# Layer 1 of a two-layer graph attention kernel: when a half block's sums are scaled and transposed

## The chip, the core and the metric

The kernel runs on one core of one Trainium2 chip. The metric is device time in microseconds (us) of one execution; of several runs the median is taken. A core has five engines that run side by side and hand work on through semaphores: TensorE (PE: matrix products, and transposes done as products), VectorE (DVE: element-wise work and reductions), ScalarE (ACT: copies with a scale, and functions such as exp), GpSimd (POOL: here mainly the issue of gathers and scatters by index) and SyncE (SP: here the issue of plain transfers). Transfers run on 16 DMA engines.

## The reference

Two graph attention layers over N = 2708 nodes with 1024 features, one adjacency matrix `adj`, and after each layer a residual sum and a layer norm:

```python
def _L1_gnn_ref(input, adj, W, a1, a2):
    h = input @ W
    f1 = h @ a1
    f2 = h @ a2
    e = jax.nn.leaky_relu(f1 + f2.T, negative_slope=0.2)
    scores = jnp.where(adj > 0, e, neg)
    attention = jax.nn.softmax(scores, axis=1)
    h_prime = attention @ h
    return jax.nn.relu(h_prime)

x = _layernorm(x + _L0_gnn_ref(x, adj, Wf, bf, Wg, bg, W0, bW))
x = _layernorm(x + _L1_gnn_ref(x, adj, W1, a1, a2))
```

Layer 0 differs in its scores (a product of two projections). The change concerns layer 1 alone. A row of `adj` has few ones, so the kernel turns it into lists of neighbours first and from then on works on listed neighbours only.

## The kernel before

**Preparation and layer 0** (lines 106 to 1105). The kernel reads `adj`, makes for each node a list of its neighbours, sorts nodes by the length of the list, and runs layer 0. Layer 0 leaves in DRAM the rows that layer 1 reads: table `T1` (1028 numbers a row: the 1024 features of layer 0's output and its product with a2's vector in column 1024) and `X1S` (the same rows as residual). The weight of layer 1 stands in `M` in SBUF.

**Layer 1: blocks, parts and tiles.** Sorted nodes form 22 blocks: one of 32 rows (20 of them real) and 21 of 128. A block of 128 has four groups of 32 rows; a *part* is half of it, two groups (`ks` = (0,1) or (2,3)). The small block is one part. That gives 43 parts, 0 to 42 here, in the order of `parts` (line 1193): part 0 is the small block, parts 2j-1 and 2j are the halves of the j-th block after it. A *tile* is one neighbour slot of one group: 128 gathered rows of T1 (526 KB). A part has 3 to 14 tiles, the last fourteen parts ten each; 405 in all.

**Gathers.** POOL issues one gather for each tile, into one of 33 slots: 20 in `ring` and 13 in `more`. The gather of tile m + 33 may go once the sums have read tile m. `Layer.gathers` (line 669) is called after each part's sums and issues those whose slots are named free then, that of the tile read last ahead of the others.

**One part, step by step.** The names are those of the profile:

- `scores1(u, ks)` (line 1137), DVE: takes column 1024 of each tile (`scores<-ring`, `scores<-more`), adds the row's own term, leaky relu and mask; then `Halves.soft` (line 776): the maximum over a row's four partitions, the difference, exp on ACT (`scores<-scores`), two multiplies that spread the weights into the stationary operand (`st<-scores,stack`), the row sums and their reciprocals (`ri`).
- `lay.sums` (line 815), TensorE: the weighted sums of the gathered rows (`po<-ring,st`, `po<-more,st`), into one of two PSUM banks in turn (`banks[:, n % 2]`).
- `lay.out` (line 839), ACT: the sums times the reciprocals, from PSUM to SBUF (`y<-po,ri`). The buffer of `y` has two copies.
- `turn_half` and `lay.turn` (lines 1207, 844): four transposes of `y` on TensorE (`pt<-ident,y`), then copies into `yT` on ACT (`yT<-pt`).
- When both halves of a block are turned, two `piece`s (line 1201) follow: half of the block's product with `M` each, eight products of 128x512 (`pm<-M,yT`; the profile counts each as two records). One part's iteration does one piece.
- `close1` (line 1157), after the second piece: SP loads the residual (`rb`, `u1b` or `u2b<-X1S`), DVE adds it to relu of the product, makes mean and variance and a Newton step for the root, ACT scales (`rb<-rb,sh,rstd`), and POOL scatters the rows to the output (`out_dram<-rb,ids`), which is issued one iteration later, ahead of that iteration's gathers.

**Order.** Each engine takes its instructions in the order in which the program names them; the class `InOrder` (line 61) holds them to it. So the order of the lines in the loop at line 1215 is the order of the queues. In iteration n it is:

- TensorE: sums(n), a piece, the transposes of part n-1
- ACT: exp(n+1), y(n), the copies of part n-1's transposes, the scale of a closing block
- DVE: scores of part n+1, the closing block's sum and norm
- POOL: the scatter of the block closed in iteration n-1, then gathers

A block whose second part is n is turned wholly in iteration n+1, has its two pieces in n+2 and n+3, closes in n+3 (an odd number) and is scattered in n+4. After the loop stand what is left: the last piece of the block before the last, the transposes of the last part, the product of the last block (`two_products`, line 557, sixteen products) and its close.

Some memsets of a small table on POOL, a count on DVE and TensorE in part 24, and the load of a flag in part 40 stand in the same loop; they serve a check of the lists' lengths.

Of the kernel before, what the change touches and what calls it, by code (L numbers as in the profile page):

```python
# [8 lines left out]
F32 = mybir.dt.float32  # L9
# [97 lines left out]
def listed_path(ctx, tc, x, adj, Wf, bf, Wg, bg, W, bW, W1, a1, a2, out):  # L107

    nc = tc.nc
    P = 128  # L110
    N, D = x.shape
    KC = D // P
    H = D // 512
# [83 lines left out]
    with tc.tile_pool(name="pre", bufs=1) as pre:  # L197
# [54 lines left out]
        with tc.tile_pool(name="adjp", bufs=3) as adjp, tc.tile_pool(name="cands", bufs=2) as cands, \  # L252
# [184 lines left out]
            steps = weights()  # L437
# [82 lines left out]
    def turn(rows, n, dst, halves=False):  # L520


        pts = []
        for k0 in range(0, KC, 4):
            pt = ps_t.tile([P, 4, P], F32, name="pt")
            at = slice(64, 64 + n) if halves and k0 and n < P else slice(0, n)
            for k in range(4):
                pe.transpose(pt[:, k, :n], rows[at, (k0 + k) * P:(k0 + k + 1) * P], ident[at, at])
            pts.append(pt)
        yield  # L530
        for k0, pt in zip(range(0, KC, 4), pts):
            if halves and k0 and n == P:
                for a, b in ((0, 64), (64, 0)):
                    act.copy(dst[:, k0:k0 + 4, a:a + 64], pt[:, :, b:b + 64])
            else:
                act.copy(dst[:, k0:k0 + 4, :n], pt[:, :, :n])
# [14 lines left out]
    def half_product(pm, h, n, xT, w, row=None):  # L551
        c = slice(h * 512, (h + 1) * 512)
        for k in range(KC):
            pe.matmul(pm[:n, h, :], xT[:, k, :n], w[:, k, c],
                      start=(row is None and k == 0), stop=(k == KC - 1))
# [43 lines left out]
    def scatter(table, idx, src):  # L599
        pool.indirect_dma_start(  # L600
            out=table, out_offset=bass.IndirectOffsetOnAxis(ap=idx, axis=0), in_=src,
            in_offset=None, bounds_check=N - 1, oob_is_err=False)

    def norm(z, n, made=None):


        st = small.tile([P, H, 6], F32, name="bst")
        mv = small.tile([P, 2], F32, name="mv")
        for h in range(H):
            if made is not None:  # L610
                made(h)
            dve.bn_stats(st[:n, h, :], z[:n, h * 512:(h + 1) * 512])
        dve.bn_aggr(mv[:n], st[:n])
        var, r, t = (small.tile([P, 1], F32, name=s) for s in ("var", "rstd", "newton"))
        dve.tensor_scalar(var[:n], mv[:n, 1:2], EPS, None, op0=ALU.add)
        ri, ti = r.bitcast(I32), t.bitcast(I32)
        dve.tensor_scalar(ti[:n], var.bitcast(I32)[:n], 1, None, op0=ALU.logical_shift_right)
        dve.tensor_scalar(ri[:n], ti[:n], -1.0, float(0x5F3759DF), op0=ALU.mult, op1=ALU.add)
        for _ in range(3):
            dve.tensor_scalar(t[:n], var[:n], r[:n], r[:n], op0=ALU.mult, op1=ALU.mult)  # L620
            dve.tensor_scalar(t[:n], t[:n], -0.5, 1.5, op0=ALU.mult, op1=ALU.add)
            dve.tensor_scalar(r[:n], r[:n], t[:n], None, op0=ALU.mult)
        sh = small.tile([P, 1], F32, name="sh")
        dve.tensor_scalar(sh[:n], mv[:n, 0:1], r[:n], -1.0, op0=ALU.mult, op1=ALU.mult)
        yield
        act.activation(z[:n, :D], z[:n, :D], AF.Identity, bias=sh[:n], scale=r[:n])
# [242 lines left out]
    with ExitStack() as s0s:  # L869
# [3 lines left out]
        stp, xp, yp, jp = (new_pool(n, 1) for n in ("stp0", "xp", "yp", "jp0"))  # L873
# [3 lines left out]
        lay = Layer(units, [ring], D, x, stp)  # L877
        xb, q, qd, F, Fr, xTs, yTs, Wp, y, Z = ({} for _ in range(10))
# [53 lines left out]
        def close(b):  # L932

            n, m, z = nrows[b], valid[b], Z.pop(b)
            pm = Wp.pop(b)

            def add(h):
                c = slice(h * 512, (h + 1) * 512)
                dve.tensor_add(z[:n, c], pm[h][:n, h, :], z[:n, c])

            if b + 1 < NB:
                dve.tensor_add(z[:n, :D], flat(pm)[:n], z[:n, :D])
            steps = norm(z, n, None if b + 1 < NB else add)
            next(steps)
            yield
            for _ in steps:
                pass
            sp.dma_start(X1S[start[b]:start[b] + m, :], z[:m, :D])
            yield
            dot(z[:n, :D], u2b, n, z[:n, D:D + 1])  # L950
            dot(z[:n, :D], u1b, n, f1[:n, b:b + 1])
            yield
            if z is not zs:
                pool.memset(z[:, D + 1:], 0.0)
            scatter(T1[:, :], ids[:m, b:b + 1], z[:m])
# [43 lines left out]
        for ks in ((0, 1), (2, 3)):  # L999
            for h in range(H):  # L1000
                c = slice(h * 512, (h + 1) * 512)
# [22 lines left out]
        closing, loaded = iter(()), 3  # L1024
        for k, u in enumerate(units):
            nxt = units[k + 1] if k + 1 < len(units) else None
            b = u.b
# [4 lines left out]
            po = ps_s.tile([P, H, 512], F32, name="po")  # L1032
# [22 lines left out]
            closing = iter(())  # L1055
# [24 lines left out]
            steps = turn(y[b], nrows[b], yT, halves=True)  # L1080
# [13 lines left out]
            if back is not None:  # L1094
                closing = close(back)
                next(closing)
        b = NB - 1
# [10 lines left out]
    with ExitStack() as s1s:  # L1108
        new_pool = lambda name, bufs: s1s.enter_context(tc.tile_pool(name=name, bufs=bufs))
        tp, yp = (new_pool(n, 2) for n in ("tp1", "yp1"))  # L1110
# [10 lines left out]
        lay = Halves(units, [ring, more], TW, T1[:, :], stp)  # L1121
# [35 lines left out]
        def close1(b, pm):  # L1157
            m, z = valid[b], x1[done1[b] % 3]
            sp.dma_start(z[:m], X1S[start[b]:start[b] + m, :])
            last = b == order1[-1]  # L1160

            def add(h):
                c = slice(h * 512, (h + 1) * 512)
                dve.scalar_tensor_tensor(z[:m, c], pm[h][:m, h, :], 0.0, z[:m, c], op0=ALU.max, op1=ALU.add)

            if not last:
                dve.scalar_tensor_tensor(z[:m], flat(pm)[:m], 0.0, z[:m], op0=ALU.max, op1=ALU.add)
            for _ in norm(z, m, add if last else None):
                pass
            yield  # L1170
            scatter(out, ids[:m, b:b + 1], z[:m])
# [4 lines left out]
        def mark_over(b):  # L1176

            for g in groups[b]:
                if g == 0:
                    for q in range(Q):  # L1180
                        pool.memset(over[32 * q:32 * q + valid[0], 0, TILES[0]:], 1.0)
                elif TILES[g] < QT:
                    pool.memset(over[:, g, TILES[g]:], 1.0)
# [10 lines left out]
        lay.gathers()  # L1194
        pool.memset(over, 0.0)
        scores1(*parts[0])
        closing, pieces, turning = iter(()), [], None
        banks = ps_s.tile([P, H, 512], F32, name="po")
        yT = {}

        def piece(b, h, pm):
            if h == 0:
                pm.append(ps_m.tile([P, H, 512], F32, name="pm"))
            half_product(pm[0], h, nrows[b], yT[b], M)
            return (b, pm[0]) if h + 1 == H else None

        def turn_half(u, ks, y):
            b = u.b
            if ks[0] == 0:
                yT[b] = tp.tile([P, KC, P], F32, name="yT")  # L1210
            steps = lay.turn(y, ks, yT[b])
            next(steps)
            return steps

        for n, (u, ks) in enumerate(parts):
            b, po = u.b, banks[:, n % 2, :]
            latest = lay.sums(u, po, ks)
            for _ in closing:
                pass
            closing = iter(())  # L1220
            lay.gathers(latest)
            made = pieces.pop(0)() if pieces else None
            steps = iter(())
            if turning is not None:
                v, kv, _ = turning
                steps = turn_half(*turning)
                if kv[-1] + 1 == v.G:
                    pm = []
                    pieces += [lambda c=v.b, h=h, pm=pm: piece(c, h, pm) for h in range(H)]
            if n + 1 < len(parts):  # L1230
                scores1(*parts[n + 1])
            y = yp.tile([P, 512], F32, name="y1")
            lay.out(u, po, ks, y)
            for _ in steps:
                pass
            turning = u, ks, y
            if ks[-1] + 1 == u.G:
                k = done1[b]
                for i in (2 * k, 2 * k + 1):
                    if i < NB:  # L1240
                        mark_over(i)
                if k == NB // 2 + 1:
                    count_over()
                if k + 2 == NB:
                    unfit = nc.values_load(flag[0:1, 0:1])
            if made is not None:
                closing = close1(*made)
                next(closing)
        while pieces:
            made = pieces.pop(0)()  # L1250
        for _ in turn_half(*turning):
            pass
        for _ in closing:
            pass
        closing = close1(*made)
        next(closing)
        prod = two_products(P, yT[b], M)
        for _ in closing:
            pass
# [366 lines left out]
```

## Time and profile before

| | us |
|---|---|
| median of 3 runs | 1890.39 |
| lowest and highest run | 1887.95, 1898.44 |
| profiled execution | 1750.29 |
| its span, first to last instruction | 1748.6 |
| layer 1's first gather starts at | 1133.72 |
| layer 1's last gather starts at | 1686.89 |
| last part's sums start at | 1700.09 |
| last scatter starts at | 1740.15 |

Of the span, PE is busy 1563.6 us (89%), DVE 1297.5 (74%), POOL 1180.9 (68%) and ACT 643.5 (37%). By stretches of layer 1, with the busy time of each engine (x: instructions), the TensorE clock that was granted, the DMA engines' busy share and what they moved in GB/s:

```
1133.00:1249.00 116.00, 89.60 (x408) 32.25 (x408) 65.30 (x326) 15.19 (x35) 88.92 (x120) 0.88 0.97 366
1249.00:1465.00 216.00, 197.97 (x955) 84.67 (x956) 126.89 (x603) 32.25 (x72) 166.77 (x222) 0.98 1.00 384
1465.00:1650.00 185.00, 169.09 (x829) 69.78 (x828) 111.70 (x531) 27.23 (x63) 141.42 (x144) 0.96 1.01 389
1650.00:1700.00 50.00, 44.55 (x200) 18.85 (x198) 27.75 (x144) 7.35 (x16) 28.64 (x29) 0.97 0.81 309
1700.00:1748.60 48.60, 33.39 (x114) 14.08 (x112) 15.97 (x52) 6.23 (x10) 2.93 (x3) 0.88 0.09 34
```

The columns after the length are PE (products), PE's weight loads, DVE, ACT and POOL.

How to read a line of the timeline: start, duration, engine, source line (all of layer 1 goes through one helper, L71, so the names of the tiles tell the instructions apart), operation, what is written and read, its shape, how many were merged, and in brackets how long the engine stood idle before and what ended that. A line of the groups has the count, then the busy time and the mean in ns, then the idle time before it and what ended that. A wait for several semaphores is put down to the one that came last. A gather's time on POOL is its issue; the transfer lands later.

### The profile page before, as it was taken

To read this page: it belongs to the slowest core of one execution; us is meant where nothing else is said; L and a number is where in the kernel's file an instruction comes from. 1 tells how busy PE (TensorE), PEld (TensorE's weight loads), DVE (VectorE), ACT (ScalarE), POOL (GpSimd) and SP (SyncE) were. 2 spreads that over 40 slices of the span, in tenths; PEclk is the share of its full clock that TensorE was granted. 3 is DMA by queue.
4 is the path that set the end of the run, shared out by engine and by line. 5 is a ranking of instruction groups with operands and counts; after the bars stand their busy time and mean duration, and the time that the engine had idled before them with its cause. 6 is when DMAs were issued, how large, how long until landed. Compare 5 with 4: busy or idle time off the path is not lost. (4 is left out here: it accounts for less than half of the span.)

```text
span 1748.6 us, 23112 instructions
## 1 busy us (share of the span) xinstructions
PE 1563.6 (89%) x6969; PEld 675.5 (39%) x6969; DVE 1297.5 (74%) x4262; ACT 643.5 (37%) x902; POOL 1180.9 (68%) x1195
## 2 busy tenths in 40 slices
PE   4999578899999999999999999559899888999896
PEld 2444233344444444444444444213344333343332
DVE  5879846899999989998999977547465555665652
ACT  4555455444444554555554444101111111111111
POOL 7888476467667767776677743177777777777740
PEclk8999778999999999999999999879999999999998
DMA  7656168578877777888887876399999999999960
GB/s 287 228 185 236 38 232 309 199 252 292 302 277 283 269 253 276 294 293 284 303 299 285 291 267 249 121 394 357 367 374 392 391 397 375 384 392 390 396 253 38
DMA packets 149986, 502.80 MB, mean 288 GB/s; under 512 B 32340, under 2 KB 32372, under 8 KB 147144
## 3 DMA queue, kind: packets, MB, share of 16 engines
q0 software_dynamic: 132032, 428.29, 66.2%
q1 hardware_dynamic: 10202, 55.72, 8.4%
q10 hardware_dynamic: 7618, 17.23, 2.7%
q8 instruction: 57, 0.93, 0.2%
q14 instruction: 77, 0.63, 0.1%
HBM read 509.64 MB, written 33.75 MB: 311 GB/s over the span
## 5 line engine op out<-in xcount | busy, mean ns | idle before, releaser
L71 POOL DMA_INDIRECT ring<-in_x_dram,SL x405 | 429.9, 1062 | 164.0 <-issue 70.0
L71 DVE SCALAR_TENSOR_TENSOR j<-ring,Fr 128x1024 bf16<-128x1024 f32 x402 | 493.9, 1229 | 41.1 <-DMA ring<-in_x_dram,SL 13.9
L71 PE MATMUL po<-ring,st 128*32 128x512 f32 x2616 | 324.4, 616 | 56.9 <-ACT y L71 32.5
L71 ACT COPY Fr<-pm 32x1024 f32<-32x1024 f32 (+2 forms) x353 | 340.6, 965 | 18.8 <-PE pm L71 14.1
L71 PE MATMUL pm<-M,yT 128*128 128x512 f32 (+1 forms) x704 | 313.3, 598 | 0.5 <-ACT yT L71 0.5
L71 PE MATMUL pm<-Wt,xT 128*128 128x512 f32 (+1 forms) x704 | 300.5, 599 | 4.7 <-DMA Wt<-in_L_gnn_W_dram 4.7
L71 POOL DMA_INDIRECT ring<-T,SL x249 | 247.0, 992 | 80.5 <-issue 66.3
L71 PE MATMUL pm<-M,xT 128*128 128x512 f32 x672 | 297.5, 601 | 0.0
L71 ACT ACTIVATE scores<-scores 128x12 f32<-128x12 f32 (+9 forms) x65 | 14.0, 216 | 631.6 <-DVE scores L71 631.6
L71 PEld LDWEIGHTS pm<-M,yT 128*128 128x128 f32 (+1 forms) x704 | 127.8, 186 | 185.0 <-issue 183.8
L71 PEld LDWEIGHTS pm<-Wt,xT 128*128 128x128 f32 (+1 forms) x704 | 131.0, 189 | 163.4 <-issue 154.6
L71 PEld LDWEIGHTS pm<-M,xT 128*128 128x128 f32 x672 | 130.2, 194 | 158.0 <-issue 155.1
L71 POOL DMA_INDIRECT more<-T,SL x156 | 154.6, 991 | 48.5 <-issue 43.8
L71 PEld LDWEIGHTS po<-ring,st 128*32 128x32 f32 x2616 | 95.9, 113 | 229.8 <-issue 174.0
L412 POOL TENSOR_TENSOR adj<-adj,iota 128x2708 f32<-128x2708 f32 (+3 forms) x23 | 130.6, 5685 | 22.7 <-ACT adj L71 22.6
L415 DVE MAX8 cand<-adj 128x8 f32<-128x136 f32 (+2 forms) x440 | 97.2, 285 | 37.4 <-POOL adj L412 37.4
L71 PE MATMUL pm<-halfT,WfT 128*128 128x512 f32 x256 | 114.1, 601 | 1.1 <-ACT WfT L71 1.1
L71 POOL DMA_INDIRECT SL<-LD,idq x85 | 86.4, 1016 | 25.8 <-issue 24.0
L71 PE MATMUL po<-more,st 128*32 128x512 f32 x624 | 82.4, 625 | 14.3 <-ACT y L71 14.3
L71 DVE TENSOR_SCALAR scores<-ring,f1q 128x4 f32<-128x4 f32 (+6 forms) x69 | 16.5, 245 | 104.1 <-DMA ring<-T,SL 93.1
L71 POOL DMA_INDIRECT z<-in_x_dram,ids x21 | 24.0, 1142 | 87.1 <-DVE j L71 36.4
L71 PEld LDWEIGHTS pm<-halfT,WfT 128*128 128x128 f32 x256 | 48.2, 193 | 58.0 <-issue 55.2
(214 smaller groups left out, 1539.5 us busy)
## 6 DMA issues: line engine op xcount, KB each, us to landing
adj<-in_adj_dram SPq DMA_DIRECT2D x21, 1354.0 KB, 5.8
X1S<-z SPq DMA_DIRECT2D x19, 512.0 KB, 5.2
ring<-in_x_dram,SL POOLq DMA_INDIRECT x405, 6.5
rows<-in_L_gnn_Wg_dram ACTq DMA_DIRECT2D x8, 512.0 KB, 4.4
rows<-in_L_gnn_Wf_dram ACTq DMA_DIRECT2D x8, 512.0 KB, 3.5
rows<-in_L_gnn_W_dram ACTq DMA_DIRECT2D x8, 512.0 KB, 6.1
Wt<-in_L_gnn_W_dram ACTq DMA_DIRECT2D x1, 4096.0 KB
M<-in_L_gnn_W_dram SPq DMA_DIRECT2D x1, 4096.0 KB
```

The source lines that it names most:

```text
L71: made = self.tc.keep_in_program_order(op(*args, **kwargs))
L412: nc.gpsimd.tensor_tensor(k[:n, cut], k[:n, cut], iota[:n, cut], op=ALU.mult)
L415: nc.vector.max(cand[:n, s, :], k[:n, s * SEG:min((s + 1) * SEG, N)])
```

## The change

The call that copies a part's sums out of PSUM (`lay.out`) moves ahead of the next part's scores, and the part's own transposes are made in the same iteration, after the piece; the variable that held a part back for the next iteration (`turning`) goes, and so does what followed the loop for it.

```diff
-        closing, pieces, turning = iter(()), [], None
+        closing, pieces = iter(()), []
...
             lay.gathers(latest)
+            y = yp.tile([P, 512], F32, name="y1")
+            lay.out(u, po, ks, y)
             made = pieces.pop(0)() if pieces else None
-            steps = iter(())
-            if turning is not None:
-                v, kv, _ = turning
-                steps = turn_half(*turning)
-                if kv[-1] + 1 == v.G:
-                    pm = []
-                    pieces += [lambda c=v.b, h=h, pm=pm: piece(c, h, pm) for h in range(H)]
+            steps = turn_half(u, ks, y)
+            if ks[-1] + 1 == u.G:
+                pm = []
+                pieces += [lambda c=b, h=h, pm=pm: piece(c, h, pm) for h in range(H)]
             if n + 1 < len(parts):
                 scores1(*parts[n + 1])
-            y = yp.tile([P, 512], F32, name="y1")
-            lay.out(u, po, ks, y)
             for _ in steps:
                 pass
-            turning = u, ks, y
...
-        while pieces:
-            made = pieces.pop(0)()
-        for _ in turn_half(*turning):
-            pass
-        for _ in closing:
-            pass
-        closing = close1(*made)
-        next(closing)
         prod = two_products(P, yT[b], M)
```

The queues of iteration n afterwards:

- TensorE: sums(n), a piece, the transposes of part n
- ACT: y(n), exp(n+1), the copies of part n's transposes, the scale of a closing block
- DVE: scores of part n+1, the closing block's sum and norm
- POOL: the scatter of the block closed in iteration n-1, then gathers

A block whose second part is n has its pieces in n+1 and n+2, closes in n+2 (an even number) and is scattered in n+3. After the loop stand the product of the last block and its close.

## The prediction

> **What bounds the kernel now.** I read the page's slices first, then the groups of layer 1, then POOL's timeline from 1133 us to the end, then TensorE's and ACT's timelines beside it. The change touches layer 1 alone, which starts with the first `ring<-T,SL` gather at 1133.72. A "part" is half a block of rows; layer 1 has 43 of them, 0 to 42.
>
> ```profile
> PE   4999578899999999999999999559899888999896
> POOL 7888476467667767776677743177777777777740
> DMA  7656168578877777888887876399999999999960
> ```
>
> From slice 27 on POOL stands at an even 7, the DMA engines at 9, TensorE between 8 and 9. An even 7 on POOL is not slack:
>
> ```profile
> L71 POOL DMA_INDIRECT ring<-T,SL x249 | 247.0, 992 | 80.5 <-issue 66.3
> L71 POOL DMA_INDIRECT more<-T,SL x156 | 154.6, 991 | 48.5 <-issue 43.8
> ```
>
> 405 gathers of 0.99 us, each followed by 0.30 us that waits for nothing: a step of 1.295 us, in POOL's timeline without a break. From the first gather (1133.72) to the last (1686.89) are 553.2 us. Between them lie 404 gathers and 18 stores of finished rows: 422 x 1.295 = 546.5; the rest, 6.7, is memsets and one gap of 1.7 us at 1667. So POOL's issue is the clock of layer 1. It is not fed late: the k-th gather after the first 33 refills the slot that the k-th tile's sums free, and by the two timelines POOL comes to a part's first refill 8.6 us (parts 11 and 25) to 30 us after those sums end.
>
> After the last gather the clock passes to TensorE:
>
> ```profile
> 1686.68 5.98 PE L71 MATMUL po<-more,st 128*32 128x512 f32 x40 [2.75 <-ACT y L71]
> 1692.59 7.13 PE L71 MATMUL pm<-M,yT 128*128 128x512 f32 x16
> 1699.56 0.60 PE L71 MATMUL pt<-ident,y 128*128 128x128 f32 x4
> ...
> 1704.52 7.13 PE L71 MATMUL pm<-M,yT 128*128 128x512 f32 x16
> 1711.49 0.60 PE L71 MATMUL pt<-ident,y 128*128 128x128 f32 x4
> 1711.92 7.03 PE L71 MATMUL pm<-M,yT 128*128 128x512 f32 x16
> 1718.79 0.60 PE L71 MATMUL pt<-ident,y 128*128 128x128 f32 x4
> 1719.86 2.41 PE L71 MATMUL pm<-M,yT 128*128 128x512 f32 x5 [0.46 <-ACT yT L71]
> ```
>
> These are sums(41), half a product of block 19 (by place in the order, block 21 is last), turn(40); then, where the dots stand, sums(42) at 1700.09; half a product of block 20, turn(41), its other half, turn(42), and the last block's products. TensorE has no gap over 0.5 us after 1686.68; the products end at 1733.9, norm, scale and store follow, and the span ends at 1748.6.
>
> Last, how an odd part starts, here part 33:
>
> ```profile
> 1574.93 0.21 ACT L71 ACTIVATE scores<-scores 128x10 f32<-128x10 f32 x1 [5.78 <-DVE scores L71]
> 1575.05 0.67 ACT L71 ACTIVATE y<-po,ri 128x512 f32<-128x512 f32 x1
> 1575.18 0.56 DVE L71 TENSOR_TENSOR st<-scores,stack 128x160 f32<-128x160 f32 x2 [0.28 <-ACT scores L71]
> 1575.77 1.85 PE L71 MATMUL po<-ring,st 128*32 128x512 f32 x12 [3.44 <-ACT y L71]
> ```
>
> The exp was late because its gather landed late; y(32), ready long before, stood behind it, and the sums began 0.05 us after y ended. By the timelines 17 of the 43 parts start just so.
>
> [...] the data follow (median 7.2 us from issue to landing). [...] 40 sum matmuls took 5.98 us after a wait of 2.75, 4.60 after one of 0.44 (part 31).
>
> **The change part by part.** No instruction is added or removed; the changed file's instruction order, built but not run, moves them.
>
> 1. The tail. A block's turn comes one part earlier, so its two half products do too. Between sums(42) and the last turn there stood a half product, a turn and another half product; afterwards there stands one half product. Removed: 1718.79 - 1711.49 = 7.30 us (7.03 product, the rest a turn, overlapped). Before sums(42) the same kinds stand as now: one half product and one turn. Over the whole layer TensorE does the same work; the moved piece goes to its start, where it waited: 2.99 us before sums(2). Parts 3 to 8 begin some 2.4 us later for that, and the wait of 5.26 us before sums(9) swallows it; POOL stands over 18 us behind there. Cost 0.
>
> 2. y before exp. An odd part starts when its first `st` multiply is done (start + 0.28 + 0.05), no longer after y: 0.27 us earlier. POOL sets the pace, so this is lost 16 times, and counts once, at sums(41): -0.27.
>
> 3. The new wait: exp(n+1) now waits for sums(n). Behind it on ACT are the copies of yT and, every second part, the closing block's scale; on DVE, which needs exp's result, the `st` multiplies. Time from the end of sums(n): y 0.7, exp 0.2, `st` 0.6, with hand-overs under 2; TensorE meanwhile has a half product and a turn, 7.5. Cost 0. If that cover were gone (as in part 0, with no half product, where the gather wait covers it) it is 1 to 2 us a part.
>
> 4. Closing on even parts, no longer odd. With sums of an odd part starting at S, DVE ends its scores at S + 1.8 (by part 41), closes a block in 5.85 (1672.94 to 1678.78), and makes the even part's scores in 3.9 (1517.33 to 1521.27): S + 11.6. TensorE comes to that part at S + 12.05 (part 31 to 32) with ten tiles, S + 13.4 in part 41. It fits by 0.45. On ACT, the close's scale (1.24) now precedes an odd part's y: that ends at S + 9.9, its turn begins at S + 11.6. Both cost 0; bounds: 0 to 2 us in the tail.
>
> 5. POOL's stores move ahead by one batch. Ahead of part 41's last gather stand 18 as before; ahead of part 42's 19, so that comes 1.3 us later (1688.2). Its landing, about 1692.8, still precedes DVE's end of the close, 1694. Cost 0. A store waits for its scale, at about S + 9.2; POOL comes to it at the end of the odd sums plus at least 8.6 less one store, S + 5 + 7 = S + 12. The fit is 3 us at the tightest, 7 mostly.
>
> SP's loads of residuals follow the closes, one part earlier, each into a buffer two closes old; the flag load on each engine left no gap in before (DVE 1688.45 to 1688.48). Cost 0.
>
> Sum: -7.30 - 0.27 = -7.6 us; profiled execution 1750.29 to 1742.7. The median of the runs, 1890.39, is 140 us above that; the page does not show what fills it. I take the same microseconds off: 1882.8 (in proportion it would be 8.2). Bounds: items 4 and 5 can take 2 back; the 1.7 us gap on POOL at 1667, which no row explains, may go or return.
>
> **The rivals.**
>
> A, the sum as worked out: 1882.8; alone 1880 to 1886.
>
> B, the tail's gain is hidden: sums(42) comes late because its scores stand behind the close on DVE, or, if the unprofiled runs have a slower TensorE (their 8% is unexplained), layer 1 is bound by TensorE, whose work is unchanged, and only the filled wait at the start counts. For it: the fit of 0.45 us. Against: part 42's lies nearer 2. Gain 3: 1887.4.
>
> C, more than the sum: the gap at 1667 goes and sums(41), with a shorter wait, run warm (5.98 to 4.60): 7.6 + 1.7 + 1.4 = 10.7: 1879.7. For it: both are in the row of the last odd part. Against: the wait there is set by data and shrinks little.
>
> D, slower: stores stall POOL. The scale is made after the odd part's scores on DVE, not right after the half product, so about 5 us later than now. If close and scale come 4 us later than worked out, each of 19 stores stops the gathers; at 1 us each 19 - 7.6 = +11: 1902. It decides from S + 12 on. Against: most batches have 7 us of room.
>
> That the change doesn't do what it says is excluded by the order of the instructions.
>
> **How the numbers follow.** A 0.56, B 0.12, C 0.22, D 0.10. About half a per cent, 9.5 us, is what a measurement of this kernel can tell from no change. A lies at 0.40% and spills over that line in a quarter of its cases (0.14); C lies beyond it. Faster 0.36, same 0.42 + 0.12 = 0.54, slower 0.10. The range, 1876 to 1889, holds A, B and most of C, and leaves D out.
>
> **What would show it.** In the profile after: one half product between sums(42) and the last turn, and the last products ending near 1726; the gathers' step still 1.295, the last issue at about 1688; odd parts starting after `st` with y far ahead; no POOL wait on ACT before the last gather. Wrong if the last gather is issued more than 2 us off 1688, if POOL's stores show a wait for `rb`, `u1b` or `u2b` before it, or if TensorE waits before sums(42).

## The result and the profile after

| | before | after |
|---|---|---|
| median of 22 runs each, us | 1892.08 | 1918.96 |
| ratio, 95% interval | | 1.0157, 1.0116 to 1.0199 |
| predicted, range, us | | 1882.8, 1876 to 1889 |
| profiled execution, us | 1750.29 | 1918.78 |
| layer 1's first gather starts, us | 1133.72 | 1204.63 |
| layer 1, from there to the end of the span, us | 614.9 | 712.4 |

The change made the kernel 26.9 us slower; the prediction had it 7.6 us faster. The ratio and its interval leave out runs more than 1.5% above the fastest of the same kernel; the medians of all 22 stand at 1.0142. The two profiled executions must not be subtracted: 70.9 us of their difference lie ahead of layer 1, where the kernels are the same. The page before is of an execution that was 142 us quicker than its kernel's median; there is no profile of the kernel before at 1892 us. So the profile after is read by itself first. From its page, the slices and two groups (busy time, mean ns, idle time before and what ended it); then two groups of its layer 1 alone:

```profile
PE   5999468689999999999999898389888977988886
POOL 8888455545677767766677741666655666666640
DMA  7646256656777877778777863989878988999960
...
L71 POOL DMA_INDIRECT ring<-T,SL x249 | 246.9, 991 | 108.1 <-issue 66.9
L71 POOL DMA_INDIRECT more<-T,SL x156 | 155.0, 993 | 66.6 <-issue 44.8
...
L71 DVE TENSOR_TENSOR st<-scores,stack 128x160 f32<-128x160 f32 (+4 forms) x85 | 23.2, 314 | 189.8 <-ACT scores L71 157.7 <-issue 30.7 <-ACT y L71 1.4
L71 PE MATMUL pt<-ident,y 128*128 128x128 f32 (+1 forms) x176 | 28.7, 287 | 48.8 <-issue 48.6
```

POOL is at a loose 5 to 6 tenths in layer 1, where it stood at an even 7: the gathers cost the same 0.99 us each, but the idle time before them is 174.7 us instead of 129.0. It is no longer the clock. Two waits are new in layer 1: TensorE before the transposes of `y` (48.8 us) and DVE before `st`, for exp (189.8 us). In the kernel before (here e9 of the experiments, 1747 us) the same groups have none and 12.1 us:

```profile
L71 PE MATMUL pt<-ident,y 128*128 128x128 f32 (+1 forms) x176 | 25.8, 271 | 0.0
L71 DVE TENSOR_TENSOR st<-scores,stack 128x160 f32<-128x160 f32 (+4 forms) x85 | 23.2, 314 | 12.1 <-ACT scores L71 12.1
```

Where they come from is seen in parts 34 and 35 (the first line is still turn(33)). TensorE's timeline, then ACT's, of the profile after:

```profile
1751.12 0.86 PE L71 MATMUL pt<-ident,y 128*128 128x128 f32 x4 [3.86 <-issue]
1751.91 1.94 PE L71 MATMUL po<-ring,st 128*32 128x512 f32 x8
1753.62 4.22 PE L71 MATMUL po<-more,st 128*32 128x512 f32 x32
1757.77 7.13 PE L71 MATMUL pm<-M,yT 128*128 128x512 f32 x16
1765.74 0.65 PE L71 MATMUL pt<-ident,y 128*128 128x128 f32 x4 [0.84 <-issue]
...
1770.86 7.13 PE L71 MATMUL pm<-M,yT 128*128 128x512 f32 x16
1781.81 0.83 PE L71 MATMUL pt<-ident,y 128*128 128x128 f32 x4 [3.82 <-issue]
```

```profile
1765.00 0.69 ACT L71 ACTIVATE y<-po,ri 128x512 f32<-128x512 f32 x1 [12.34 <-PE pm L71]
1765.59 0.20 ACT L71 ACTIVATE scores<-scores 128x10 f32<-128x10 f32 x1
...
1781.07 0.69 ACT L71 ACTIVATE y<-po,ri 128x512 f32<-128x512 f32 x1 [5.46 <-remote]
1781.65 0.20 ACT L71 ACTIVATE scores<-scores 128x10 f32<-128x10 f32 x1
```

The sums of part 34 end at 1757.84 by the record, and its reciprocals were made at 1753.87; yet y(34) starts at 1765.00, 7.2 us later, and y(35) 10.2 us after sums(35) (1770.92). TensorE has by then finished its half product and waits for y, 0.84 us in the one part and 3.82 in the other. The view says `issue` of these waits, that is, it found no update that ended them; many updates of ACT are missing from this trace (399 stand in it, 538 in e8's). But after each of the 21 such waits in layer 1 the transposes start 0.05 us after a y has ended. The trace also holds the times at which semaphores were updated. For TensorE's own, in us (ends of sums by the record; the first column of times is worked out from the matmul records):

```
             sums end   TensorE's next update    y starts
part 34       1757.84         1764.93             1765.00
part 35       1770.92         1780.99             1781.07
part 36       1788.53         1795.63             1795.70
part 37       1801.63         1811.65             1811.74
```

In the trace the last product of a part's sums carries an update of TensorE's semaphore (in 42 of 43 parts), and y waits for that semaphore in these four. Some of TensorE's updates are missing too, so that the next one in the trace need not be that of the sums; but y starts 0.07 to 0.09 us after each of these four. So the update came 7.1 to 10.1 us after the recorded end. That the record puts the end too early does not explain it: the sums can't have run so long, since the half product behind them and the transposes, whose copies on ACT start 0.03 us after their recorded end (1782.67), had no room left: from 1780.99 to 1782.65 are 1.66 us, and the half product alone takes 7.13.

POOL waits for TensorE's signals as well, and for ACT's scales. Its timeline, at a store of an earlier block and at the start of the gathers after sums(35), and DVE's, at the close of the block that is stored:

```profile
1391.20 1.02 POOL L71 DMA_INDIRECT out_dram<-u1b,ids  x1 [9.80 <-ACT u1b L71]
...
1781.25 1.01 POOL L71 DMA_INDIRECT ring<-T,SL  x1 [2.10 <-remote]
```

```profile
1383.81 1.22 DVE L71 SCALAR_TENSOR_TENSOR u1b<-pm,u1b 128x1024 f32<-128x1024 f32 x1 [7.71 <-remote]
```

The half product that DVE reads there ended at 1370.84 by the record; the update came at 1383.78, 12.9 us later, and the close, its scale on ACT (1389.68) and POOL's store behind it follow from that. The stores ahead of the last gather waited 46.9 us for their scales, six of them for more than 2 us each.

### The profile page after: what moved, and what is told of

Read it like the earlier page. It is cut to its first block, busy times and chain, and to the rows that moved or that the text cites. A ratio compares the mean times of both kernels' runs of the same rounds, so it can differ in the third digit from the quotient of the medians.

```text
span 1917.0 us, 23104 instructions
## 1 busy us (share of the span) xinstructions
PE 1647.7 (86%) x6969; PEld 692.6 (36%) x6969; DVE 1291.6 (67%) x4262; ACT 645.5 (34%) x902; POOL 1200.6 (63%) x1195
## 4 chain that ended last, share of the span: by engine, by line
PE 35%; issue 9%; DVE 7%; DMA 4%; POOL 1%; another core or an unknown queue 1%; ACT 0%; POOLq 0%; DVEq 0%; ACTq 0%
PE pm L71 20%; PE po L71 13%; DVE j L71 4%; DMA ring<-in_x_dram,SL 3%; PE pt L71 2%; POOL ring L71 1%; DVE newton L71 1%; DVE bst L71 0%; DMA z<-in_x_dram,ids 0%; DVE z L71 0%; DVE rstd L71 0%; DMA T<-ring,ids 0%; DMA ring<-T,SL 0%; DVE mq L71 0%
## 5 line engine op out<-in xcount | busy, mean ns | idle before, releaser
L71 POOL DMA_INDIRECT ring<-in_x_dram,SL x405 | 447.3, 1104 | 222.3 <-issue 97.7
L71 PE MATMUL po<-ring,st 128*32 128x512 f32 x2616 | 361.9, 623 | 60.8 <-issue 46.9
L71 PE MATMUL pm<-M,yT 128*128 128x512 f32 (+1 forms) x704 | 321.3, 607 | 12.9 <-issue 12.2
L71 PE MATMUL pm<-M,xT 128*128 128x512 f32 x672 | 304.0, 609 | 9.1 <-issue 9.1
L71 PEld LDWEIGHTS pm<-M,yT 128*128 128x128 f32 (+1 forms) x704 | 128.4, 187 | 207.9 <-issue 206.7
L71 PEld LDWEIGHTS po<-ring,st 128*32 128x32 f32 x2616 | 107.7, 114 | 257.5 <-issue 232.9
L71 DVE TENSOR_TENSOR st<-scores,stack 128x128 f32<-128x128 f32 (+9 forms) x122 | 41.2, 377 | 210.9 <-ACT scores L71 178.6
L71 ACT ACTIVATE y<-po,ri 128x512 f32<-128x512 f32 (+1 forms) x88 | 58.0, 683 | 299.2 <-remote 124.7
L412 POOL TENSOR_TENSOR adj<-adj,iota 128x2708 f32<-128x2708 f32 (+3 forms) x23 | 130.5, 5682 | 22.3 <-ACT adj L71 22.2
L71 PE MATMUL po<-more,st 128*32 128x512 f32 x624 | 102.6, 685 | 17.9 <-issue 17.7
L71 PE MATMUL pt<-ident,y 128*128 128x128 f32 (+1 forms) x352 | 51.3, 279 | 51.1 <-issue 50.1
```

The costliest lines, as they stand in the source:

```text
L71: made = self.tc.keep_in_program_order(op(*args, **kwargs))
L412: nc.gpsimd.tensor_tensor(k[:n, cut], k[:n, cut], iota[:n, cut], op=ALU.mult)
```

## The experiments

**Two kinds of sets.** A set is a group of kernels that were run together on one chip. The kernel before took 1746.5 to 1750.6 us (medians) in the sets on four chips and 1893.2 in the set on a fifth. By its times the result's set is of the second kind, the page before of the first. TensorE's granted clock is lower in the second kind (for the kernel before 0.94 at the median of e4's set, against 0.96), but the median half product takes 7.13 us in the profiles of both, so a slower clock as such is not the difference. Below, "1748 set" and "1892 set" mean these. The expectations name four theories: N, nothing in the changed order is slow by itself, but a loop (sums, y, transposes and exp, next sums) costs where the signals of sums come late; L, that loop costs always; T, the transposes that wait for their own `y` are all of it; C, closes and stores that come one part earlier are.

**The kernel before again, and the two halves of the change** (1748 set). e1 is the kernel before. e2 moves `lay.out` alone:

```diff
             lay.gathers(latest)
+            y = yp.tile([P, 512], F32, name="y1")
+            lay.out(u, po, ks, y)
             made = pieces.pop(0)() if pieces else None
...
                 scores1(*parts[n + 1])
-            y = yp.tile([P, 512], F32, name="y1")
-            lay.out(u, po, ks, y)
             for _ in steps:
                 pass
             turning = u, ks, y
```

e3, against the changed kernel, puts exp ahead of y again:

```diff
             lay.gathers(latest)
-            y = yp.tile([P, 512], F32, name="y1")
-            lay.out(u, po, ks, y)
             made = pieces.pop(0)() if pieces else None
+            if n + 1 < len(parts):
+                scores1(*parts[n + 1])
+            y = yp.tile([P, 512], F32, name="y1")
+            lay.out(u, po, ks, y)
             steps = turn_half(u, ks, y)
...
-            if n + 1 < len(parts):
-                scores1(*parts[n + 1])
```

> The kernel before, unchanged, for a second profile: the one on the page was 140 us quicker than the median, and the profile of the changed kernel has stretches in which TensorE gets one instruction in 1.4 to 2.8 us, in both layers. All theories expect these stretches here too, layer 1 starting near 1200 us, and a time within 1% of 1892. Theory L (a loop through y): in layer 1 the signal of a part's last sum matmul comes within 0.1 us of its recorded end, as in the first profile, or late as in the changed kernel; if late, ACT's y shows it and TensorE doesn't wait for it. POOL stands behind the sums by several us in most parts.

> Half of the change: y(n) goes ahead of exp(n+1), but part n is still turned one part later, so closes and stores stay on the parts where they were. Theory L: most of the loss is here, since st(n+1) and so sums(n+1) now stand behind y(n) and the signal of sums(n): ratio 1.010 (1.005 to 1.015), DVE's st waiting over 100 us for ACT in layer 1. Theory C (closes and stores one part earlier stall POOL and ACT): 1.000. Theory T (the transposes waiting for their own y on TensorE): 1.000.

> The other half: part n is turned in its own iteration, as in the changed kernel, with its closes and stores on even parts, but exp(n+1) stays ahead of y(n). Theory L: exp and st are free of the signal of sums(n), TensorE waits only where y is late, the tail's 7.3 us are won: ratio 0.997 (0.993 to 1.003). Theory C: 1.015, as the whole change. Theory T: 1.010 to 1.015, with TensorE idle 1 to 4 us before the transposes.

Measured: before 1748.97; e1 1753.0; e2 1749.09, ratio 1.0000 (0.9985 to 1.0015); e3 1739.08, 0.9936 (0.9911 to 0.9961). My expectation of e1 failed: its trace has no stretches of one instruction at a time, and layer 1 starts at 1137, not near 1200. y ahead is worth nothing, the turn at once 10 us. Both halves are harmless here, so T and C, which had asked 1.010 or more of e3, fall for this set, and so does L's 1.010 for e2. The groups of layer 1 of e3 show how little a wait may mean:

```profile
L71 PE MATMUL po<-ring,st 128*32 128x512 f32 x996 | 137.0, 649 | 16.6 <-DVE rs L71 16.6
L71 PE MATMUL pt<-ident,y 128*128 128x128 f32 (+1 forms) x176 | 29.2, 292 | 38.1 <-ACT y L71 37.9
```

TensorE waits 38.1 us before the transposes (48.8 in the result's profile), and the kernel is faster than before: the wait has come out of the 63 us that TensorE stood before sums in the kernel before (e9), for POOL paces the layer (0.99 us a gather, 129.6 us idle before all of them, 128.4 in e9).

**The whole change and e3 side by side** (1892 set).

> The changed kernel again. In the last set the kernel before took 1749 us, in the set of the result 1892: two chips, or two states of one. Theory N (nothing in the order of the change is slow by itself; the loop sums, y, turn costs only where TensorE's signals come late, as in the set of the result): beside a kernel before of about 1749 the ratio is 0.994 to 0.997 and the signals of sums come within 0.1 us; beside one of about 1890 it is 1.014 (1.010 to 1.020) and they come up to 10 us late. Theory L (the loop costs by itself): 1.008 or more in both, TensorE waiting 0.8 to 3.9 us before the transposes.

> The turn at once with exp(n+1) left ahead of y(n), again, beside the changed kernel. If the kernel before takes about 1749: 0.994 as in the last set. If it takes about 1890: theory N and theory L, 0.990 to 1.004, since st(n+1) doesn't stand behind y(n) and TensorE waits for y(n) only before the turn; theory T (TensorE's wait for its own y is the whole loss): 1.012 to 1.018, as the changed kernel.

Measured: before 1893.23; e4, the changed kernel, 1922.84, 1.0188 (1.0045 to 1.0331); e5, the kernel of e3, 1903.41, 1.0079 (1.0046 to 1.0111). So both orders lose here, e3's though it gained 0.6% in the 1748 set. e4 lies in the range of theory N, e5 above it (0.990 to 1.004): N had not foreseen a loss with exp ahead of y. A third (medians: 10.2 of 29.6 us) to a half (ratios: 0.8 of 1.6 to 1.9%) of the loss remains so. The ratios' intervals overlap, but every run of e5 (1878.2 to 1912.8 us) is quicker than every one of e4 (1913.2 to 1929.2). Groups of layer 1 in e5:

```profile
L71 PE MATMUL pt<-ident,y 128*128 128x128 f32 (+1 forms) x176 | 31.9, 311 | 59.0 <-issue 52.6 <-ACT y L71 6.0
L71 DVE TENSOR_TENSOR st<-scores,stack 128x160 f32<-128x160 f32 (+4 forms) x85 | 23.3, 315 | 20.5 <-ACT scores L71 11.5 <-ACT yT L71 4.8 <-issue 4.2
```

The wait of `st` for exp is gone (20.5 us; 189.8 in layer 1 of the result's profile); the wait before the transposes is not. Stores waited 22 us for their scales ahead of the last gather, against 46.9 in the result's profile and 59.4 in e4. But e5's layer 1 (698.5 us; 720.9 in e4's) is not shorter by its waits: before transposes and before the first product of sums TensorE stood 76 us in e5 and 65 in e4. The sums themselves, from first to last product, take 256 us in place of 289; the idle time before their products that the view puts down to `issue` is 16.4 us in place of 50.8 (the last section shows such a stretch). What exp's place has to do with that, one profile of each does not tell.

**The whole change in a 1748 set.**

> The kernel before, unchanged, once more, for a profile in a set in which it takes about 1890 us. There: theory N expects the signals of sums late by several us here too (y of the parts that don't wait for their exp starting 1 to 10 us after the sums' recorded end), TensorE going on meanwhile, since neither exp(n+1), st(n+1) nor the transposes of the part before need that signal, and under 1 us of idle time before the transposes in all of layer 1; layer 1 takes 685 to 695 us. Theory L: signals prompt (0.1 us), so that the late signals come from the changed order. If the set takes about 1750: as the first repeat.

> y ahead of exp alone, again. If the kernel before takes about 1890: theory N, 1.006 to 1.014, since exp(n+1), st(n+1) and sums(n+1) stand behind the late signal of sums(n), while the transposes are those of the part before and don't; theory T (the transposes waiting for their own y are the loss): 1.000. If it takes about 1750: 1.000 as before.

> The changed kernel beside the other two. If the kernel before takes about 1890: 1.016 (1.012 to 1.020) as twice before. If it takes about 1750: theory N, 0.994 to 0.997 (tail 7.3 us and a little), signals of sums prompt and no wait over 0.5 us before the transposes; theory L: 1.008 or more.

Measured: before 1746.53; e6, the kernel before, 1743.98; e7, as e2, 1.0005 (0.9991 to 1.0019); e8, the changed kernel, 1738.80, 0.9957 (0.9943 to 0.9971): 7.7 us faster. That settles L: the changed order has no cost of its own in such a set. TensorE's end in e8:

```profile
1690.56 0.62 PE L71 MATMUL po<-more,st 128*32 128x512 f32 x2 [0.39 <-DVE st L71]
...
1695.21 7.13 PE L71 MATMUL pm<-M,yT 128*128 128x512 f32 x16
1702.18 0.60 PE L71 MATMUL pt<-ident,y 128*128 128x128 f32 x4
1703.24 14.00 PE L71 MATMUL pm<-M,yT 128*128 128x512 f32 x32 [0.46 <-ACT yT L71]
```

The first line is the start of sums(42). One half product stands between them and the last turn, and from the start of sums(42) to the end of the span (1731.9) are 41.3 us; in the kernel before they were 48.5. Signals are prompt: sums that end at 1520.58 have their update at 1520.62. The wait before the transposes is 1.0 us in all of layer 1.

**A late y made on purpose** (1748 set). Before y(n), ACT reads one element of the half product of the same iteration, in the changed kernel (e11) and in the kernel before (e12):

```diff
             half_product(pm[0], h, nrows[b], yT[b], M)
+            fresh.append(pm[0][0:1, h, 0:1])
...
+            while fresh:
+                act.copy(seen[0:1, 0:1], fresh.pop())
             y = yp.tile([P, 512], F32, name="y1")
             lay.out(u, po, ks, y)
```

(In e11 the `pieces.pop` line stands ahead of these; TensorE's order is the same.) e9 and e10 repeat the kernel before and y ahead.

> The kernel before, for a profile in a set where it takes about 1890 us (the last two repeats fell in sets of about 1749). If it does: theory N expects signals of sums late by several us here too, with TensorE under 1 us idle in all before the transposes of layer 1, and layer 1 at 685 to 695 us; theory L prompt signals (0.1 us).

> y ahead of exp alone, for a set of about 1890: theory N 1.006 to 1.014; theory T 1.000. In a set of about 1749: 1.000 as twice before.

> The changed kernel in which y(n) is made late on purpose: ACT first reads one element of the half product that follows sums(n), so y(n) can't start before that product ends, as in most parts of the set of the result. Nothing else is moved. In a set of about 1749, where signals are prompt: if a late y closes the loop through the transposes and exp (theory N), TensorE stands about 1.1 us (read 0.2, y 0.7, hand-overs) before the transposes in each of 40 parts, 44 us in all, of which part comes out of its waits for st: 1.000 to 1.015 of the kernel before, at least 8 us more than the 1739 of the changed kernel, and ACT's wait for the product takes the place of that for sums. If the order alone is harmless even with a late y: 0.996 as the changed kernel. In a set of about 1890: as the changed kernel there, 1.012 to 1.022.

> The same read of the half product ahead of y(n) in the kernel before, after exp(n+1). There the transposes of part n come a part later and exp stands ahead of y, so a late y is behind nothing: theory N 1.000 (0.998 to 1.003) in either kind of set. If a late y costs by itself (ACT's copies and scales behind it): 1.005 or more.

Measured: before 1747.80; e9 1747.08; e10 0.9991 (0.9979 to 1.0003); e11 1742.30, 0.9969 (0.9955 to 0.9983); e12 1748.28, 1.0002 (0.9985 to 1.0018). I had asked of theory N at least 8 us above the changed kernel; e11 lies 3.5 above e8, and still below the kernel before. TensorE does wait 37.8 us before the transposes, as meant, but its waits before sums fall from 51.4 us (e8) to 22.1. DVE waits 130.5 us for exp before `st`, and that costs nothing visible either. A late y alone is not enough: N as I had put it falls.

**A late y with TensorE as the bound** (1748 sets). In the result's profile TensorE has nothing to take a wait out of: from part 2 on no sums wait before their first product (in e8 51.4 us of waits in all), and it was busy 582.7 us in layer 1 where e8's was 535.9. To make TensorE the bound, 109 us of products were added, to the kernel before without (e17) and with the read of e12 (e14), to the changed kernel without (e16) and with the read of e11 (e15):

```diff
+            for k in range(3):
+                pe.matmul(pm[0][:nrows[b], h, :], yT[b][:, k, :nrows[b]], M[:, k, h * 512:(h + 1) * 512], start=True, stop=True)
             half_product(pm[0], h, nrows[b], yT[b], M)
```

e13 and e18 are the kernel before, for a profile in an 1892 set.

> The kernel before, for a profile in a set in which it takes about 1890 us. If it does: signals of sums late by several us here too (theory N), under 1 us idle in all before the transposes of layer 1, layer 1 at 685 to 695 us, the gathers no longer in a row without a break. If it takes about 1748: as the three before.

> The kernel before with y(n) held until the end of the half product (as e12) and with TensorE made the bound: ahead of each half product three of its eight products are made once more into the same place, 3 x 0.89 = 2.7 us in 41 parts, 109 us in all, where TensorE waits 63 us in layer 1 now (ten tiles: 12.3 + 2.7 = 15.0 us of TensorE a part against 13.6 of POOL). All theories, in a set of about 1748: 1.030 to 1.045, TensorE's waits for sums and transposes in layer 1 falling under 30 us.

> The changed kernel with both: y(n) held until the end of the half product (as e11), and the same 109 us of products. Theory N (a late y costs in the changed order once TensorE is the bound, since it then stands before the transposes about 1.1 us in each of 40 parts): 1.010 to 1.025 above e14, that is 20 to 40 us, with 40 to 60 us before the transposes. Theory L as for e11 (the order hides a late y): 7 us below e14. In a set of about 1890: above e14 by at least 1.010 too.

> The changed kernel with the 109 us of products, y not held. If TensorE as the bound is enough to make the change a loss: 1.010 above e14. Theory N: a prompt y makes it none, 0.993 to 0.998 of e14 (about 7 to 10 us below it), under 5 us before the transposes.

> The kernel before with the 109 us of products and y not held, the missing partner of e16. e14 (y held) stood 32 us above e16, where I had written 7 to 10: sums(n+1) of the kernel before waits for y(n) as well, 0.44 us a part in e14. If that is it, 25 us of e14 go when y is prompt, and this kernel lies 7 to 10 us above e16's 1788: 1.026 to 1.030 of the kernel before in a set of about 1748, with no wait for y before the sums beyond 5 us in all. If TensorE as the bound makes the change worth more by itself: above 1.033.

> The kernel before once more, for a profile in a set in which it takes about 1890 us, as e13: signals of sums late by several us (theory N), TensorE under 1 us idle before the transposes of layer 1 but some 0.4 us a part before the sums, which wait for y(n) too.

Measured (us; waits are TensorE's idle time in layer 1, from the groups):

| | time | ratio to before | wait before sums | before transposes |
|---|---|---|---|---|
| e17: before, busy | 1798.38 | 1.0280 (1.0259 to 1.0301) | 26.1 | 0.0 |
| e16: after, busy | 1788.30 | 1.0228 (1.0194 to 1.0263) | 20.6 | 1.0 |
| e14: before, busy, late y | 1820.72 | 1.0404 (1.0368 to 1.0441) | 42.5 | 0.0 |
| e15: after, busy, late y | 1846.84 | 1.0574 (1.0533 to 1.0615) | 20.7 | 37.8 |

e13 and e18 took 1745.62 and 1745.54: both fell in 1748 sets. With TensorE as the bound and a prompt y the changed order gains 10.1 us (e16 and e17 stood in different sets; by the ratios it is 0.5%, and their intervals just touch). With a late y it loses 26.1 us (e15 against e14, one set; N had said 20 to 40). That this is also the size of the result is luck: how much work was added and how late y was made are my choices, not the 1892 set's. The late y costs the kernel before 22.3 us and the changed one 58.5. Four expectations missed: e14's waits are above 30 us, e15's before the transposes below the 40 to 60 written, e16 lies 1.8% below e14 where 0.2 to 0.7 was written, and sums of e17 still wait 9.2 us for y. In e15 POOL's stores wait 93 us for their scales (29 in e14), but TensorE shows no wait for gathered rows: before sums it stands 3.6 us for `st`, the rest is the layer's start. TensorE's timelines show a part each, e14, e15 and e16:

```profile
1645.88 0.60 PE L71 MATMUL pt<-ident,y 128*128 128x128 f32 x4
1646.91 1.16 PE L71 MATMUL po<-ring,st 128*32 128x512 f32 x8 [0.44 <-ACT y L71]
1647.80 3.71 PE L71 MATMUL po<-more,st 128*32 128x512 f32 x32
1651.44 9.71 PE L71 MATMUL pm<-M,yT 128*128 128x512 f32 x22
1660.99 0.60 PE L71 MATMUL pt<-ident,y 128*128 128x128 f32 x4
```

```profile
1640.94 0.66 PE L71 MATMUL pt<-ident,y 128*128 128x128 f32 x4 [0.88 <-ACT y L71]
1641.52 1.16 PE L71 MATMUL po<-more,st 128*32 128x512 f32 x8
1642.40 3.71 PE L71 MATMUL po<-ring,st 128*32 128x512 f32 x32
1646.05 9.71 PE L71 MATMUL pm<-M,yT 128*128 128x512 f32 x22
1656.63 0.66 PE L71 MATMUL pt<-ident,y 128*128 128x128 f32 x4 [0.88 <-ACT y L71]
```

```profile
1654.42 0.60 PE L71 MATMUL pt<-ident,y 128*128 128x128 f32 x4
1654.95 4.50 PE L71 MATMUL po<-ring,st 128*32 128x512 f32 x40
1659.38 9.71 PE L71 MATMUL pm<-M,yT 128*128 128x512 f32 x22
1668.93 0.60 PE L71 MATMUL pt<-ident,y 128*128 128x128 f32 x4
```

From one turn to the next are 15.11 us in e14, 15.69 in e15 and 14.51 in e16. In the kernel before the transposes are those of the part before and run while y is made, so only what is left of y, 0.44 us, holds the next sums (which wait for y(n) although they write the other bank); in the changed one y holds the transposes, and these the sums: 1.18 us a part, twice the 0.60. So it is shown that a late y, where TensorE has no room, turns the change from a gain into a loss. That this is what happened in the result's set is argued from the two waits in its profile, not shown.

## Why the prediction was wrong

**The step that failed** is item 3, the new wait: "Cost 0", with a cover of 7.5 us. Two things in it were wrong. It listed exp, the copies, the scale and `st` as what stands behind y(n), and left out the transposes of part n, which the change puts behind it on TensorE. It counted the turn as part of the cover, but the turn itself waits. The real cover is the half product, 7.13 us, and it lasts only while y starts promptly after the sums. With prompt signals both slips cost nothing: in e8 TensorE waits 1.0 us before transposes in the whole layer. The term that failed is the hand-over. I put the hand-overs at "under 2" with the y and the rest; where signals are prompt they are 0.04 us to the update and 0.12 to y's start (e8, sums that end at 1532.51, y at 1532.63), but in the result's set the update alone took 7 to 10 us in the parts shown (median of all parts 6.5, as far as updates are recorded). The item priced the loss of the cover at 1 to 2 us a part; e15 against e16 shows 1.2, and the result's profile 0.84 and 3.82 by turns.

**The second failure** is the transfer, "I take the same microseconds off". The 140 us between the page and the median were named as unexplained, and then taken as if they lay beside the change. They did not lie beside it. In the changed kernel's profile 70.9 us of such a difference lie ahead of layer 1, the rest within it, and there POOL no longer paces the layer and TensorE has lost its room before the sums.

**What held**, where the page's kind of set was met (e8): -7.6 us were predicted, -7.7 measured (5 to 10 by the interval, so that the closeness is in part luck). The tail term, -7.30, measured 48.5 - 41.3 = 7.2. The last gather was to come 1.3 us later; from the layer's first gather it came at 554.7 (1126.10 to 1680.75) instead of 553.2, 1.5 later. y ahead of exp, -0.27, is not told from nothing (e2, e7, e10). The close on even parts, cost 0 with a fit of 0.45 us: sums(42) did wait 0.39 us for `st`. Stores did not stop the gathers, although POOL's room was smaller than read: in the timelines before, the first refill comes 5.3 us after the sums of part 9 (1262.06 to 1267.38) and 5.9 after those of part 25, not 8.6 at the least. In the result's profile two of the three signs of being wrong came true: the last gather was issued at 1850.35, and stores waited for their scales.

**The rivals.** B had the right cause in half: it named a slower TensorE in the other runs, which would make TensorE the bound. But it took the work as unchanged and so the loss as none, and e16 against e17 shows that TensorE as the bound is not enough. D had the right sign and a visible trace: in the result's profile stores did stop POOL, for 46.9 us. But its reason, a scale made behind the odd part's scores on DVE, is not what happened: in e8, with the same order of closes, no store before the last gather stands longer than 0.31 us. In the result's profile the close itself began 13 us late, for want of the half product's signal. Here the stops follow from the late signals; the stores' place alone makes none.

**What stays open.** How much of the loss is the waits before the transposes. In the result's profile layer 1 is 106.6 us longer than in e8's. By the matmul records TensorE's sums, from first to last product, take 66 us more (275 against 209), 61 of it in six parts held up as in the last section; half products take 19 more; the waits before transposes are 48 longer, those before the first product of sums 30 shorter. So the parts that are held up weigh more here than the waits that the change makes. The kernel before probably has them too: if the work ahead of layer 1 takes as long as in the changed kernel's profile, its own layer 1 at the median takes about 686 us (1892.1 - 1.7 - 1204.6, an estimate), 71 more than on the page. But no profile shows it, nor how late its signals are. e5 says that y ahead of exp is half of the loss or more, but not by which wait; y ahead alone (e2, e7, e10) never met an 1892 set. POOL's stops held no sums visibly, as none waited before their first product after part 1. And why the signals are late was not tried.

## What to carry to other kernels

Before a producer's result is consumed sooner, ask how much slack the consumer had, and whether the page shows the kind of execution that the median is made of: a gap between profile and median is part of the kernel, and a change must be worked out once with every engine in turn as the bound. Taking a stage's pipelining away (here one part between y and its transposes) gains the length of that stage once, at the end, and pays in every round for a delay of the hand-over that the other engine has no room to hide: here 7 us once, against waits of 0.7 to 4.9 us in eighteen parts. An order that beats the kernel before on one chip (e3, 0.9936) can lose to it on another (e5, 1.0079); neither of the two orders that were measured in both kinds of sets beat the kernel before in both.

## What the hardware showed unexpectedly

- One kernel takes 1747 us in sets on four chips and 1893 in one on a fifth; whether this lies in the chip itself is not shown. In the three profiles of the longer kind TensorE waits 44.6 to 59.0 us before the transposes (1.0 in e8), and 16.4 to 53.9 us before products of sums with no wait that the view names (0.3 at most in e8). In the result's profile its semaphore updates are late (median 6.5 us, as far as recorded), and there are stretches in which it gets one instruction at a time (1.27 to 1.52 us idle before each of three):

```profile
1841.83 1.45 PE L71 MATMUL po<-ring,st 128*32 128x512 f32 x7
1844.55 0.59 PE L71 MATMUL po<-ring,st 128*32 128x512 f32 x1 [1.27 <-issue]
1846.65 0.69 PE L71 MATMUL po<-ring,st 128*32 128x512 f32 x1 [1.52 <-issue]
1848.74 1.01 PE L71 MATMUL po<-ring,st 128*32 128x512 f32 x1 [1.40 <-issue]
```

- In that stretch DVE gets its instructions singly too (four of them after 1.24 to 1.68 us idle), while POOL goes on issuing a gather every 1.3 us. After it signals were prompt again: the update of the sums that ended at 1868.43 came at 1868.47. The same holds of stretches in the middle of the layer: sums(21) took 17.4 us (6.8 in e8), their update came after 0.02 us, and that of sums(22) was 9.5 us late again.
- The trace of the same program holds 2560 updates of DVE's semaphore and 603 of TensorE's in e8, but 1773 and 525 in the result's profile (1826 and 528 in e4's). Whether the recording has to do with the late signals no run shows; an execution without it was not made.
